# A four-layer graph network on one core: norm statistics aggregated on GpSimd, two additions turned into transfers, softmax masks and sums in operations of 1024 columns

## The chip, the core and the metric

The kernel runs on one core of a Trainium2 chip. The core has five engines that run side by side, each in the order of its own instructions, and wait for one another through semaphores. The profile calls them PE (TensorE, the matrix multiplier; PEld is its weight load), DVE (VectorE), ACT (ScalarE), POOL (GpSimd) and SP (which only issues transfers here). Transfers (DMA) are moved by 16 DMA engines; they are issued from SP or from POOL. The metric is the time on the device from the first to the last instruction of the core, in microseconds (us), as the median of the runs.

## The reference, cut to what matters

The input is 64 graphs of 256 nodes with 256 features each, and an adjacency matrix of 256 x 256 whole numbers for each graph. Four layers follow one another; around each there is a residual and a norm without gain or shift.

```python
x = _layernorm(x + transformer(x, adj))   # layer 0: 8 heads, masked softmax, feed-forward of 1024
x = _layernorm(x + gat1(x, adj))          # layer 1: graph attention
x = _layernorm(x + gat2(x, adj))          # layer 2: graph attention, then elu
x = _layernorm(x + relational(x, adj))    # layer 3: two graph convolutions

def transformer(x, adj, ...):
    qkv = x @ Wqkv.T + bqkv
    scores = jnp.where(allowed, (q * scale) @ k.T, -jnp.inf)
    attn = jax.nn.softmax(scores, axis=-1)
    x = _layernorm(x + (attn @ v) @ Wo.T + bo, ln1_g, ln1_b)
    ff = jax.nn.relu(x @ W1.T + b1) @ W2.T + b2
    return _layernorm(x + ff, ln2_g, ln2_b)

def _layernorm(x, axis=-1, eps=1e-5):
    m = jnp.mean(x, axis=axis, keepdims=True)
    v = jnp.var(x, axis=axis, keepdims=True)
    return (x - m) / jnp.sqrt(v + eps)
```

So there are six norms a graph: two in the transformer and one at the end of each layer. All is computed in 32-bit floating point.

## The kernel before

The program is built from small steps ("ops"). Each has an engine, an estimated cost, tiles that it reads and writes, and tiles come from rings of a fixed number of buffers. A list scheduler in the kernel file plays the ops of all 64 graphs through with these costs, and writes each engine's instructions in the order that comes out. About seven graphs are in flight at once: a graph's output leaves some 310 us after its input was transposed. `port="uses"` marks a VectorE op with two operands in SBUF; `port="waits"` marks a GpSimd op that the scheduler does not start while such an op runs. `lag` is the time from the end of an op to when its result is seen. `PERIOD` spaces the dates by which the graphs are due.

```python
RINGS = {..., "p": 12, "both": 4, "X": 8, "h": 3, "e": 3, "o": 4, ...}
class Plan:
    PERIOD = 46.0

def with_row(xt, row, op, reads=()):             # VectorE: xt op= row, 512 columns
    dve(0.60, lambda: nc.vector.tensor_tensor(xt(), xt(), row[:, None, :].to_broadcast([P, NB, D]), op=op), ...)

def add_later(xt, yt, reads):                    # a transfer that adds: issued by GpSimd
    op("POOL", 0.6, lambda: nc.gpsimd.dma_start(xt(), yt(), accum_op=ALU.add), [xt, *reads], [xt], lag=3.0)

def add(xt, yt):                                 # VectorE: xt += yt, 512 columns
    dve(0.60, lambda: nc.vector.tensor_tensor(xt(), xt(), yt(), op=ALU.add), [xt, yt], [xt], "uses")
```

The norm, used six times a graph. VectorE makes statistics of the two node tiles (`bn_stats`) and aggregates them to mean and variance (`bn_aggr`), GpSimd makes scale and shift of them in four small operations, and ScalarE applies these.

```python
def layer_norm(y):
    def stats():
        for i in range(NB):                      # NB = 2
            nc.vector.bn_stats(stat()[:, i, :], y()[:, i, :])
        for i in range(NB):
            nc.vector.bn_aggr(mv()[:, i, :], stat()[:, i, :])
    def root():
        nc.gpsimd.tensor_scalar(rstd()[:, 0, :], mv()[:, :, 1], 1.0, EPS, op0=ALU.mult, op1=ALU.add)
        nc.gpsimd.tensor_tensor(rstd()[:, 0, :], rstd()[:, 0, :], neghalf[:, 0:NB], op=ALU.pow)
        nc.gpsimd.tensor_tensor(rstd()[:, 1, :], mv()[:, :, 0], rstd()[:, 0, :], op=ALU.mult)
        nc.gpsimd.tensor_scalar(rstd()[:, 1, :], rstd()[:, 1, :], -1.0, 1.0, op0=ALU.mult, op1=ALU.mult)
    def apply():
        for i in range(NB):
            nc.scalar.activation(y()[:, i, :], y()[:, i, :], AF.Identity, bias=..., scale=...)
    dve(0.88, stats, [y], [mv, stat])
    op("POOL", 1.6, root, [mv], [rstd], port="waits", lag=0.4)
    act(1.0, apply, [y, rstd], [y])
```

The attention. For each half of the keys (`kt`) TensorE makes four banks of scores, one for each `r`, with two heads of 256 columns in a bank. ScalarE takes the exponential of a bank, VectorE multiplies it by the mask and later adds the two halves for the softmax sums.

```python
for kt in range(NB):
    ...                                          # scores of this half: 16 matmuls into 4 banks
    for r in range(4):
        act(0.58, lambda ...: nc.scalar.activation(pr(), sr(), AF.Exp, accum_out=...), [s[r]], [pr])
        dve(0.60, lambda ...: nc.vector.tensor_tensor(
            pr(), pr(), am()[:, kt, None, :].to_broadcast([P, KB, N]), op=ALU.mult), [pr, am], [pr], "uses")
for r in range(4):
    dve(0.60, lambda r=r: nc.vector.tensor_tensor(both[r](), p[0, r](), p[1, r](), op=ALU.add), ...)
for hg in range(KB):                             # sums (ones x both) and values (v x p): TensorE
    pe("col", 1.32, values, [v] + both + list(p.values()), [pc], [ctxT, inv])
    ...                                          # reciprocal of the sums and a product: VectorE
```

The feed-forward and the end of a graph:

```python
x1T = transposed(x1)                             # TensorE and ScalarE
with_row(x1, ln1g, ALU.mult)
with_row(x1, b2, ALU.add)                        # b2 here is ln1_b + b2
...                                              # x1T x W1, relu, x W2: 32 matmuls of 256 columns
y = product_plus(..., w2, NF, x1)                # VectorE adds x1 to the product
...
h = conv(conv(xt, 0, rel, rdeg), 1, rel, rdeg)
add(h, xt)                                       # the last residual
layer_norm(h)
op("SP", 0.4, lambda: nc.sync.dma_start(out_graph[g], h()), [h], [])
```

Of the kernel before, what the change touches and what calls it, by code (L numbers as in the profile page):

```python
# [12 lines left out]
AF = mybir.ActivationFunctionType  # L13
ALU = mybir.AluOpType
# [3 lines left out]
P = 128  # L18
EPS = 1e-5
# [5 lines left out]
SENT, BACK = 3.0, 4.5  # L25


RINGS = {"x": 3, "adj": 4, "bits": 2, "am": 2, "gm": 6, "T": 4, "qk": 2, "v": 2, "p": 12, "both": 4, "inv": 1, "ctxT": 2, "X": 8,
         "xr": 1, "hid": 1, "h": 3, "e": 3, "n": 1, "rel": 3, "hi": 2, "lo": 2, "o": 4, "blocks": 1, "turned": 1, "xT": 2}
DRAM = {"rows": 6}  # L30
SMALL = {"mv": 8, "st": 4, "rstd": 8, "r": 6, "rdeg": 4}
# [23 lines left out]
class Plan:  # L55
# [8 lines left out]
    TO = {"PE": 0.06, "POOL": 0.05}  # L64
    NEXT = {"DVE": 0.1}
    SWITCH = 0.1
    PERIOD = 46.0
    LAST, SPACE = 5, 0.1

    def __init__(self):  # L70
# [142 lines left out]
def tile_gnn_stack(ctx: ExitStack, tc: tile.TileContext, t: dict, out: bass.AP):  # L213
# [16 lines left out]
    nc = tc.nc  # L230
# [4 lines left out]
    KB = D // P  # L235
# [250 lines left out]
    def main_path(plan):  # L486
# [86 lines left out]
        def graph(g):  # L573
            def op(engine, cost, issue, reads, writes, takes=(), mode=None, port=None, lag=None):
                plan.op(engine, cost, issue, g, reads, writes, takes, mode, port, lag)

            def pe(mode, cost, issue, reads, writes, takes=()):
                op("PE", cost, issue, reads, writes, takes, mode)

            def dve(cost, issue, reads, writes, port=None):  # L580
                op("DVE", cost, issue, reads, writes, port=port)

            def act(cost, issue, reads, writes):
                op("ACT", cost, issue, reads, writes)

            def new(ring, shape, dtype=F32):
                return plan.tile(ring, shape, dtype)
# [9 lines left out]
            def with_row(xt, row, op, reads=()):  # L597
                dve(0.60, lambda: nc.vector.tensor_tensor(xt(), xt(), row[:, None, :].to_broadcast([P, NB, D]), op=op),
                    [xt, *reads], [xt], "uses")
# [8 lines left out]
            def add(xt, yt):  # L608
                dve(0.60, lambda: nc.vector.tensor_tensor(xt(), xt(), yt(), op=ALU.add), [xt, yt], [xt], "uses")
# [48 lines left out]

            def layer_norm(y):

                mv, stat = new("mv", [P, NB, 2]), new("st", [P, NB, 6])
                rstd = new("rstd", [P, 2, NB])

                def stats():
                    for i in range(NB):
                        nc.vector.bn_stats(stat()[:, i, :], y()[:, i, :])  # L666
                    for i in range(NB):
                        nc.vector.bn_aggr(mv()[:, i, :], stat()[:, i, :])  # L668

                def root():  # L670
                    nc.gpsimd.tensor_scalar(rstd()[:, 0, :], mv()[:, :, 1], 1.0, EPS, op0=ALU.mult, op1=ALU.add)  # L671
                    nc.gpsimd.tensor_tensor(rstd()[:, 0, :], rstd()[:, 0, :], neghalf[:, 0:NB], op=ALU.pow)  # L672
                    nc.gpsimd.tensor_tensor(rstd()[:, 1, :], mv()[:, :, 0], rstd()[:, 0, :], op=ALU.mult)
                    nc.gpsimd.tensor_scalar(rstd()[:, 1, :], rstd()[:, 1, :], -1.0, 1.0, op0=ALU.mult, op1=ALU.mult)  # L674

                def apply():
                    for i in range(NB):
                        nc.scalar.activation(y()[:, i, :], y()[:, i, :], AF.Identity, bias=rstd()[:, 1, i : i + 1],  # L678
                                             scale=rstd()[:, 0, i : i + 1])
# [29 lines left out]
            def projections(xT):  # L709
# [22 lines left out]
                act(0.47, lambda: nc.scalar.copy(v(), pv()), [pv], [v])  # L732
                return qk, v

            def attention(xT, am):

                qk, v = projections(xT)
                ctxT = new("ctxT", [P, KB, N])  # L740
                p = {}
                for kt in range(NB):
                    s = [new("bank", [P, KB, N]) for r in range(4)]
                    for r in range(4):
                        p[kt, r] = new("p", [P, KB, N])
# [8 lines left out]
                    pe("row", 0.97, scores, [qk], s, [p[kt, r] for r in range(4)])  # L754
                    for r in range(4):
                        pr, k = p[kt, r], 8 * g + 4 * kt + r
                        act(0.58, lambda pr=pr, k=k, sr=s[r]: nc.scalar.activation(  # L757
                            pr(), sr(), AF.Exp, accum_out=seen_sum[:, k : k + 1]), [s[r]], [pr])
                        dve(0.60, lambda pr=pr, kt=kt: nc.vector.tensor_tensor(  # L759
                            pr(), pr(), am()[:, kt, None, :].to_broadcast([P, KB, N]), op=ALU.mult), [pr, am], [pr], "uses")  # L760
                both = [new("both", [P, KB, N]) for r in range(4)]
                for r in range(4):
                    dve(0.60, lambda r=r: nc.vector.tensor_tensor(both[r](), p[0, r](), p[1, r](), op=ALU.add),  # L763
                        [p[0, r], p[1, r]], [both[r]], "uses")
                inv = new("inv", [P, KB, N])
                for hg in range(KB):
                    pc = new("bank", [P, 2, N])

                    def values(hg=hg, pc=pc):
                        for r in range(4):  # L770
                            nc.tensor.matmul(pc()[32 * r : 32 * r + 32, 1, :], lhsT=ones, rhs=both[r]()[:, hg, :],  # L771
                                             start=True, stop=True)
                        for kt in range(NB):
                            for r in range(4):
                                h = 4 * hg + r
                                nc.tensor.matmul(pc()[32 * r : 32 * r + 32, 0, :], lhsT=v()[:, kt, HD * h : HD * (h + 1)],  # L776
                                                 rhs=p[kt, r]()[:, hg, :], start=(kt == 0), stop=(kt == NB - 1))

                    pe("col", 1.32, values, [v] + both + list(p.values()), [pc], [ctxT, inv])
# [443 lines left out]
```

## Time and profile before

| what | value |
|---|---|
| median of 3 runs | 2897.77 us (2897.14 to 2898.14) |
| profiled execution | 2897.1 us |
| mean granted clock of TensorE | 0.991 of full speed |
| instructions with a place in the program | 50588 |
| transfers | 278.32 MB, 96 GB/s on average |

In the profile an engine's busy time is the time that is covered by its instructions, and its idle time before an instruction is put down to whatever ended last of what the instruction waited for. A row of a group of instructions gives line, engine, operation, the tile that is written and the tiles that are read, shapes (partitions x columns), the count, the sum of busy time, the mean of one in nanoseconds, and the idle time before them with what ended it. A row of the waits gives who waited for whom, the sum in us, how many times, and the longest. A row of a table of windows gives the stretch from the start of the span, its length, then the busy time of each engine in it with the count of instructions, the granted clock, the busy share of the DMA engines and GB/s. The chain of waits is followed back from the last instruction and is told in order of time: start, length, what. A matmul of 32-bit numbers is two matmul instructions in the profile. Instructions of one engine overlap somewhat in the records, so that the mean of one times the count can exceed the busy time.

### The profile page before, as it was taken

To read this page: it belongs to the slowest core of one execution; us is meant where nothing else is said; L and a number is where in the kernel's file an instruction comes from. 1 tells how busy PE (TensorE), PEld (TensorE's weight loads), DVE (VectorE), ACT (ScalarE), POOL (GpSimd) and SP (SyncE) were. 2 spreads that over 40 slices of the span, in tenths; PEclk is the share of its full clock that TensorE was granted. 3 is DMA by queue.
4 is the path that set the end of the run, shared out by engine and by line. 5 is a ranking of instruction groups with operands and counts; after the bars stand their busy time and mean duration, and the time that the engine had idled before them with its cause. 6 is when DMAs were issued, how large, how long until landed. Compare 5 with 4: busy or idle time off the path is not lost.

```text
span 2897.1 us, 50588 instructions
## 1 busy us (share of the span) xinstructions
PE 2805.3 (97%) x16182; PEld 2128.1 (73%) x16182; DVE 2523.0 (87%) x6557; ACT 1540.4 (53%) x3713; POOL 789.1 (27%) x1685
## 2 busy tenths in 40 slices
PE   8999999999999999999999999999999999999975
PEld 6776777777777767777777777777777777777853
DVE  6879899989989898999889898899888998999686
ACT  3555555546455555655555465555555655555343
POOL 2232223222223222222222322232231332222221
PEclk9999999999999999999999999999999999999998
DMA  7454455445444444454444544444444544443342
GB/s 183 81 108 88 99 101 102 89 101 102 95 92 100 87 94 94 98 101 93 104 97 93 98 99 99 100 91 102 86 93 96 109 88 93 105 90 72 67 83 70
DMA packets 844512, 278.32 MB, mean 96 GB/s; under 512 B 692656, under 2 KB 810672, under 8 KB 844240
## 3 DMA queue, kind: packets, MB, share of 16 engines
q1 hardware_dynamic: 808800, 240.27, 37.7%
q0 software_dynamic: 35440, 34.76, 8.5%
q8 instruction: 131, 2.15, 0.3%
q14 instruction: 141, 1.16, 0.1%
HBM read 157.43 MB, written 83.89 MB: 83 GB/s over the span
## 4 chain that ended last, share of the span: by engine, by line
PE 82%; DVE 10%; ACT 3%; DMA 2%; issue 2%; POOL 1%; SPq 1%; DVEq 0%; POOLq 0%; ACTq 0%
PE bank L657 67%; PE bank L919 4%; PE bank L776 3%; PE bank L751 3%; PE bank L771 2%; DMA rows<-turned 2%; DVE p L759 1%; PE bank L618 1%; DVE turned L629 1%; PE bank L839 1%; SPq L633 1%; DVE st L666 1%; DVE o L929 1%; DVE both L763 1%; DVE e L844 1%
## 5 line engine op out<-in xcount | busy, mean ns | idle before, releaser
L671 POOL TENSOR_SCALAR rstd<-mv 128x2 f32<-128x2 f32 x384 | 104.4, 272 | 1869.8 <-DVE mv L668 1496.7
L678 ACT ACTIVATE X<-X,rstd 128x256 f32<-128x256 f32 x640 | 349.8, 597 | 244.7 <-POOL rstd L674 230.1
L657 PE MATMUL bank<-cw,T 128*128 128x512 f32 x1024 | 467.9, 600 | 9.6 <-DMA T<-rows 9.1
L657 PE MATMUL bank<-T,w 128*128 128x256 f32 x2048 | 471.6, 380 | 5.2 <-ACT p L757 2.6
L657 PE MATMUL bank<-w,hid 128*128 128x256 f32 x2048 | 460.1, 380 | 0.0
L657 PEld LDWEIGHTS bank<-w,hid 128*128 128x128 f32 x2048 | 385.9, 190 | 62.7 <-issue 10.4
L657 PEld LDWEIGHTS bank<-T,w 128*128 128x128 f32 x2048 | 382.7, 190 | 64.5 <-issue 6.9
L757 ACT ACTIVATE p<-bank 128x512 f32<-128x512 f32 x512 | 299.9, 598 | 87.8 <-PE bank L751 87.6
L657 PEld LDWEIGHTS bank<-cw,T 128*128 128x128 f32 x1024 | 192.2, 192 | 209.3 <-issue 195.2
L759 DVE TENSOR_TENSOR p<-p,am 128x512 f32<-128x512 f32 x512 | 332.8, 680 | 10.8 <-ACT p L757 10.7
L672 POOL TENSOR_TENSOR rstd<-rstd,neghalf 128x2 f32<-128x2 f32 x384 | 305.7, 796 | 32.1
L809 ACT ACTIVATE hid<-bank,col_b 128x256 f32<-128x256 f32 x512 | 209.4, 474 | 113.8 <-PE bank L657 112.1
L657 PE MATMUL bank<-xT,wqkv 128*128 128x256 f32 x1024 | 251.6, 387 | 13.4 <-DVE xT L650 12.9
L657 PE MATMUL bank<-h,e 128*128 128x259 f32 x1024 | 253.8, 388 | 11.0 <-ACT e L849 9.3
L657 PE MATMUL bank<-gw,T 128*128 128x258 f32 x1024 | 249.1, 384 | 2.1 <-ACT inv L783 1.5
L657 PEld LDWEIGHTS bank<-h,e 128*128 128x128 f32 x1024 | 192.7, 192 | 66.6 <-issue 19.3
L666 DVE BATCH_NORM_STATS2 st<-X 128x6 f32<-128x256 f32 x640 | 237.5, 413 | 1.8
L906 ACT CAST hi<-bank 128x256 fp32r<-128x256 f32 x256 | 94.6, 370 | 263.4 <-PE bank L657 262.6
L657 PEld LDWEIGHTS bank<-xT,wqkv 128*128 128x128 f32 x1024 | 189.7, 192 | 54.0 <-issue 13.5
L780 DVE RECIPROCAL inv<-bank 128x256 f32<-128x256 f32 x128 | 220.0, 1734 | 8.8 <-PE bank L776 8.6
L657 PEld LDWEIGHTS bank<-gw,T 128*128 128x128 f32 x1024 | 191.1, 191 | 36.7 <-issue 5.2
L629 DVE STREAM_TRANSPOSE turned<-X 128x512 f32<-128x512 f32 x192 | 134.9, 703 | 45.0 <-DMA rows<-turned 23.0
(121 smaller groups left out, 4775.4 us busy)
## 6 DMA issues: line engine op xcount, KB each, us to landing
rows<-turned SPq DMA_DIRECT2D x1024, 64.0 KB, 2.2
T<-rows SPq DMA_DIRECT2D x256, 256.0 KB, 2.8
adj<-in_adj_dram SPq DMA_DIRECT2D x128, 256.0 KB, 3.0
blocks<-in_x_dram SPq DMA_DIRECT2D x512, 32.0 KB, 2.3
x<-in_x_dram SPq DMA_DIRECT2D x64, 256.0 KB, 3.0
xr<-in_x_dram SPq DMA_DIRECT2D x64, 256.0 KB, 2.8
xr<-row_ln_b POOLq DMA_DIRECT2D x64, 256.0 KB, 4.4
x<-row_bo POOLq DMA_DIRECT2D x64, 256.0 KB, 4.8
```

The source lines that it names most:

```text
L629: dve(0.63, lambda: nc.vector.transpose(turned().rearrange("p b q n -> p (b q n)"), xt().rearrange("p i (k b c) -> p b (i k) c", k=KB, b=4 ...
L657: nc.tensor.matmul(dst, lhsT=lhs(c), rhs=rhs(c), start=(c == 0), stop=(c == n - 1))
L666: nc.vector.bn_stats(stat()[:, i, :], y()[:, i, :])
L671: nc.gpsimd.tensor_scalar(rstd()[:, 0, :], mv()[:, :, 1], 1.0, EPS, op0=ALU.mult, op1=ALU.add)
L672: nc.gpsimd.tensor_tensor(rstd()[:, 0, :], rstd()[:, 0, :], neghalf[:, 0:NB], op=ALU.pow)
L678: nc.scalar.activation(y()[:, i, :], y()[:, i, :], AF.Identity, bias=rstd()[:, 1, i : i + 1], scale=rstd()[:, 0, i : i + 1])
L757: act(0.58, lambda pr=pr, k=k, sr=s[r]: nc.scalar.activation(pr(), sr(), AF.Exp, accum_out=seen_sum[:, k : k + 1]), [s[r]], [pr])
L759: dve(0.60, lambda pr=pr, kt=kt: nc.vector.tensor_tensor(pr(), pr(), am()[:, kt, None, :].to_broadcast([P, KB, N]), op=ALU.mult), [pr, am] ...
L780: dve(1.62, lambda hg=hg, pc=pc: nc.vector.reciprocal(inv()[:, hg, :], pc()[:, 1, :]), [pc], [(inv, hg)])
L809: act(0.36, lambda f=f, k=k, ph=ph: nc.scalar.activation(hid()[:, f + k, :], ph()[:, k, :], AF.Relu, bias=b1[:, f + k : f + k + 1]), [ph, ...
L906: act(0.27, lambda i=i, po=po: nc.scalar.copy(hi()[:, i, 0:D], po()[:, D:]), [po], [(hi, i)])
L919: nc.tensor.matmul(pa()[:, 0:n], lhsT=rel()[:, i, j * P : (j + 1) * P], rhs=part()[:, i, 0:n], start=(c == 0), stop=(c == len(terms) - 1))
```

## The change

The change takes work off VectorE in three ways.

The norm's two `bn_aggr` are left out. `bn_stats` leaves, for the even and the odd half of a row, a count, a mean and a sum of squared deviations; GpSimd now combines the halves itself, in nine small operations where there were four.

Two additions become transfers that add in place, issued by GpSimd: the row b2 onto x1 in the feed-forward, and the last residual, except in the last two graphs.

The masks and the sums of the softmax are made for two banks at a time: the tiles p and both hold twice as much, there are half as many of them, and each VectorE operation covers 1024 columns and not 512. The exponentials still come a bank at a time.

The scheduler's costs are set to the new shapes, and PERIOD goes from 46 to 47. No matmul is added or removed.

```diff
-RINGS = {... "p": 12, "both": 4, ...}
+RINGS = {... "p": 6, "both": 2, ...}
-    PERIOD = 46.0
+    PERIOD = 47.0
             def layer_norm(y):
-                mv, stat = new("mv", [P, NB, 2]), new("st", [P, NB, 6])
-                rstd = new("rstd", [P, 2, NB])
+                stat, t, rstd = new("st", [P, NB, 2, 3]), new("mv", [P, NB, 4]), new("rstd", [P, 2, NB])
                 def stats():
                     for i in range(NB):
-                        nc.vector.bn_stats(stat()[:, i, :], y()[:, i, :])
-                    for i in range(NB):
-                        nc.vector.bn_aggr(mv()[:, i, :], stat()[:, i, :])
+                        nc.vector.bn_stats(stat()[:, i].rearrange("p h k -> p (h k)"), y()[:, i, :])
                 def root():
...
+                    tensor_tensor(t()[:, :, 0:2], stat()[:, :, 0, 1:3], stat()[:, :, 1, 1:3], op=ALU.add)
+                    tensor_tensor(d, stat()[:, :, 0, 1], stat()[:, :, 1, 1], op=ALU.subtract)
+                    tensor_tensor(d, d, d, op=ALU.mult)
+                    tensor_scalar(s, s, 4 / D, 4 * EPS, op0=ALU.mult, op1=ALU.add)
+                    tensor_tensor(d, d, s, op=ALU.add)
+                    tensor_tensor(d, d, neghalf[:, 0:NB], op=ALU.pow)
+                    tensor_tensor(shift, m, d, op=ALU.mult)
+                    tensor_scalar(shift, shift, -1.0, 1.0, op0=ALU.mult, op1=ALU.mult)
+                    tensor_scalar(scale, d, 2.0, 1.0, op0=ALU.mult, op1=ALU.mult)
...
-                dve(0.88, stats, [y], [mv, stat])
-                op("POOL", 1.6, root, [mv], [rstd], port="waits", lag=0.4)
+                dve(0.56, stats, [y], [stat])
+                op("POOL", 2.5, root, [stat], [t, rstd], port="waits", lag=0.6)
...
-                        act(0.58, lambda pr=pr, k=k, sr=s[r]: nc.scalar.activation(
-                            pr(), sr(), AF.Exp, accum_out=seen_sum[:, k : k + 1]), [s[r]], [pr])
-                        dve(0.60, lambda pr=pr, kt=kt: nc.vector.tensor_tensor(
-                            pr(), pr(), am()[:, kt, None, :].to_broadcast([P, KB, N]), op=ALU.mult), [pr, am], [pr], "uses")
+                        act(0.58, lambda pr=pr, j=j, k=k, sr=s[r]: nc.scalar.activation(
+                            pr()[:, j], sr(), AF.Exp, accum_out=seen_sum[:, k : k + 1]), [s[r]], [(pr, j)])
+                        if j == 1:
+                            dve(1.14, lambda pr=pr, kt=kt: nc.vector.tensor_tensor(
+                                heads(pr), heads(pr), am()[:, kt, None, :].to_broadcast([P, 2 * KB, N]), op=ALU.mult),
+                                [pr, am], [pr], "uses")
-                both = [new("both", [P, KB, N]) for r in range(4)]
-                for r in range(4):
-                    dve(0.60, lambda r=r: nc.vector.tensor_tensor(both[r](), p[0, r](), p[1, r](), op=ALU.add),
+                for r in (0, 2):
+                    both[r] = new("both", [P, 2, KB, N])
+                    dve(1.14, lambda r=r: nc.vector.tensor_tensor(heads(both[r]), heads(p[0, r]), heads(p[1, r]), op=ALU.add),
...
-                with_row(x1, b2, ALU.add)
+                add_row_later(x1, b2)
...
-            add(h, xt)
+            if g < B - 2:
+                add_later(h, xt, [xt])
+            else:
+                add(h, xt)
             layer_norm(h)
```

More of the change, by code (lines that the diff above doesn't have):

```diff
@@ L25 @@
 SENT, BACK = 3.0, 4.5
-RINGS = {"x": 3, "adj": 4, "bits": 2, "am": 2, "gm": 6, "T": 4, "qk": 2, "v": 2, "p": 12, "both": 4, "inv": 1, "ctxT": 2, "X": 8,
+RINGS = {"x": 3, "adj": 4, "bits": 2, "am": 2, "gm": 6, "T": 4, "qk": 2, "v": 2, "p": 6, "both": 2, "inv": 1, "ctxT": 2, "X": 8,
          "xr": 1, "hid": 1, "h": 3, "e": 3, "n": 1, "rel": 3, "hi": 2, "lo": 2, "o": 4, "blocks": 1, "turned": 1, "xT": 2}
@@ L659, in layer_norm @@
             def layer_norm(y):
-                mv, stat = new("mv", [P, NB, 2]), new("st", [P, NB, 6])
-                rstd = new("rstd", [P, 2, NB])
+                stat, t, rstd = new("st", [P, NB, 2, 3]), new("mv", [P, NB, 4]), new("rstd", [P, 2, NB])
                 def stats():
                     for i in range(NB):
-                        nc.vector.bn_stats(stat()[:, i, :], y()[:, i, :])
-                    for i in range(NB):
-                        nc.vector.bn_aggr(mv()[:, i, :], stat()[:, i, :])
+                        nc.vector.bn_stats(stat()[:, i].rearrange("p h k -> p (h k)"), y()[:, i, :])
                 def root():
[L671 to L674, printed above, removed]
+                    tensor_tensor, tensor_scalar = nc.gpsimd.tensor_tensor, nc.gpsimd.tensor_scalar
+                    m, s, d = t()[:, :, 0], t()[:, :, 1], t()[:, :, 2]
+                    scale, shift = rstd()[:, 0, :], rstd()[:, 1, :]
+                    tensor_tensor(t()[:, :, 0:2], stat()[:, :, 0, 1:3], stat()[:, :, 1, 1:3], op=ALU.add)
[7 more added lines that the diff above has]
+                    tensor_scalar(scale, d, 2.0, 1.0, op0=ALU.mult, op1=ALU.mult)
                 def apply():
@@ L733, in projections, with heads @@
                 return qk, v
+            def heads(t):
+                return t().rearrange("p r k n -> p (r k) n")
             def attention(xT, am):
@@ L743, in attention @@
                     s = [new("bank", [P, KB, N]) for r in range(4)]
-                    for r in range(4):
-                        p[kt, r] = new("p", [P, KB, N])
+                    for r in (0, 2):
+                        p[kt, r] = new("p", [P, 2, KB, N])
                     def scores(kt=kt, s=s):
@@ L752, in scores @@
                                                  rhs=qk()[f, hg, :], start=True, stop=True)
-                    pe("row", 0.97, scores, [qk], s, [p[kt, r] for r in range(4)])
+                    pe("row", 0.97, scores, [qk], s, [p[kt, 0], p[kt, 2]])
                     for r in range(4):
-                        pr, k = p[kt, r], 8 * g + 4 * kt + r
-                        act(0.58, lambda pr=pr, k=k, sr=s[r]: nc.scalar.activation(
-                            pr(), sr(), AF.Exp, accum_out=seen_sum[:, k : k + 1]), [s[r]], [pr])
-                        dve(0.60, lambda pr=pr, kt=kt: nc.vector.tensor_tensor(
-                            pr(), pr(), am()[:, kt, None, :].to_broadcast([P, KB, N]), op=ALU.mult), [pr, am], [pr], "uses")
-                both = [new("both", [P, KB, N]) for r in range(4)]
-                for r in range(4):
-                    dve(0.60, lambda r=r: nc.vector.tensor_tensor(both[r](), p[0, r](), p[1, r](), op=ALU.add),
+                        pr, j, k = p[kt, r - r % 2], r % 2, 8 * g + 4 * kt + r
+                        act(0.58, lambda pr=pr, j=j, k=k, sr=s[r]: nc.scalar.activation(
[4 more added lines that the diff above has]
+                                [pr, am], [pr], "uses")
+                both = {}
+                for r in (0, 2):
+                    both[r] = new("both", [P, 2, KB, N])
+                    dve(1.14, lambda r=r: nc.vector.tensor_tensor(heads(both[r]), heads(p[0, r]), heads(p[1, r]), op=ALU.add),
                         [p[0, r], p[1, r]], [both[r]], "uses")
@@ L770, in values @@
                         for r in range(4):
-                            nc.tensor.matmul(pc()[32 * r : 32 * r + 32, 1, :], lhsT=ones, rhs=both[r]()[:, hg, :],
+                            nc.tensor.matmul(pc()[32 * r : 32 * r + 32, 1, :], lhsT=ones, rhs=both[r - r % 2]()[:, r % 2, hg, :],
                                              start=True, stop=True)
@@ L776, in values @@
                                 nc.tensor.matmul(pc()[32 * r : 32 * r + 32, 0, :], lhsT=v()[:, kt, HD * h : HD * (h + 1)],
-                                                 rhs=p[kt, r]()[:, hg, :], start=(kt == 0), stop=(kt == NB - 1))
-                    pe("col", 1.32, values, [v] + both + list(p.values()), [pc], [ctxT, inv])
+                                                 rhs=p[kt, r - r % 2]()[:, r % 2, hg, :], start=(kt == 0), stop=(kt == NB - 1))
+                    pe("col", 1.32, values, [v, *both.values(), *p.values()], [pc], [ctxT, inv])
                     dve(1.62, lambda hg=hg, pc=pc: nc.vector.reciprocal(inv()[:, hg, :], pc()[:, 1, :]), [pc], [(inv, hg)])
```

## The prediction

> **What bounds the kernel now.** I began with the page: busy shares, then the 40 slices.
>
> ```profile
> PE 2805.3 (97%) x16182; PEld 2128.1 (73%) x16182; DVE 2523.0 (87%) x6557; ACT 1540.4 (53%) x3713; POOL 789.1 (27%) x1685
> ...
> PE   8999999999999999999999999999999999999975
> ...
> DVE  6879899989989898999889898899888998999686
> ```
>
> TensorE is busy from the second slice to the 38th. VectorE, from which the change takes work, has eights and nines, but is not the fuller of the two. A busy TensorE need not be an efficient one, so I took the starts of its matmuls between 100 and 2700 us from the trace: a 128x256 matmul follows its predecessor by a median of 216 ns in all the large groups, and by 215 to 226 ns on average. What lies above the median in these groups sums to about 60 us, a few ns at each change of group. Matmuls stream; hardly any waits are hidden in the busy share. Next, the middle and the end as two windows (start and end, length, busy us of PE, PEld, DVE, ACT, POOL, clock, DMA share, GB/s):
>
> ```profile
> 100.00:2700.00 2600.00, 2570.24 (x15041) 1955.43 (x15035) 2325.29 (x6016) 1426.73 (x3459) 723.61 (x1536) 1.00 0.47 95
> 2700.00:2898.00 198.00, 149.11 (x574) 103.21 (x572) 133.65 (x410) 75.15 (x155) 39.11 (x102) 0.91 0.36 74
> ```
>
> This is the reading on which most rests. In the middle TensorE idles for 2600 - 2570 = 30 us, 1.1%. In the last 198 us it idles for 49, and in the first 100 for 14 (one wait of 12.9 us for the first transposed input, which the change leaves as it is). These 93 us are all the idle time there is. Who ends it in the middle is told by the waits of TensorE there (sum, count, longest):
>
> ```profile
> PE bank L657 <- ACT p L757: 7.2, 8, 1.6
> PE bank L839 <- DVE h L830: 3.4, 1, 3.4
> PE bank L771 <- DVE both L763: 3.1, 5, 1.2
> ```
>
> Small, rare, of many kinds; VectorE ends some directly and stands behind others. The end is different: there the chain runs through VectorE, ScalarE, transfers and short matmuls in turn. Its last norm shows the part that the change rebuilds:
>
> ```profile
> 2888.13 0.49 DVE st L666 x2
> 2888.62 0.18 issue
> 2888.80 0.31 DVE mv L668 x2
> 2889.15 0.10 issue
> 2889.26 0.20 POOL rstd L671
> 2889.46 0.07 issue
> 2889.53 0.71 POOL rstd L672
> ```
>
> L668 is the aggregation that goes; each small GpSimd operation takes 0.20 us and 0.07 of issue, the power 0.71.
>
> **What the Trainium skill says.** (1) "Trainium Kernel Development and Optimization", section Performance Expectations: matmul busy time is a bad measure of the distance to the roofline, because matmuls are pipelined. The trace agrees in part: one matmul is recorded at 380 ns where 216 pass to the next. So I used the pace for the middle. (2) "VectorE: DVE Perf Modes", section Why `tensor_tensor` can't do 2×_2P or 4×: both read ports are taken, so 32-bit operations on two tensors gain no speed from length, only one fixed cost. The rows below agree: 413 ns at 256 columns, 680 at 512. (3) "GPSIMD Engine Reference", section 8, Key points: GpSimd shares its SBUF interfaces with VectorE and contends with VectorE instructions that have two SBUF inputs. The trace agrees: single durations of L673 have a median of 197 ns but a 90th percentile of 602, and in the timeline such an operation ends where a VectorE operation on two SBUF tensors ends. (4) "DMA: Bandwidth & Descriptors", section Rules for kernel authors: a transfer that accumulates is to be issued from GpSimd. Here all adding transfers stand in GpSimd's queue; each takes it 1.3 us and lands after 4.4 to 4.8.
>
> **The change, part by part.** The groups:
>
> ```profile
> L759 DVE TENSOR_TENSOR p<-p,am 128x512 f32<-128x512 f32 x512 | 332.8, 680 | 10.8 <-ACT p L757 10.7
> L763 DVE TENSOR_TENSOR both<-p 128x512 f32<-128x512 f32 x256 | 167.5, 681 | 0.0
> L668 DVE BATCH_NORM_AGGREGATE mv<-st 128x2 f32<-128x6 f32 x768 | 115.5, 174 | 1.0
> L875 DVE SCALAR_TENSOR_TENSOR n<-n,X 128x256 f32<-128x256 f32 x128 | 53.0, 414 | 0.0
> L598 DVE TENSOR_TENSOR X<-X,row_b 128x512 f32<-128x512 f32 x64 | 43.7, 682 | 0.1
> L609 DVE TENSOR_TENSOR o<-o,X 128x512 f32<-128x512 f32 x64 | 43.6, 682 | 0.2
> L671 POOL TENSOR_SCALAR rstd<-mv 128x2 f32<-128x2 f32 x384 | 104.4, 272 | 1869.8 <-DVE mv L668 1496.7 <-DVE r L854 127.0 <-ACT p L757 61.7
> L672 POOL TENSOR_TENSOR rstd<-rstd,neghalf 128x2 f32<-128x2 f32 x384 | 305.7, 796 | 32.1
> ```
>
> VectorE loses: the aggregations, 115.5 us. The b2 row, 43.7. The last residual in 62 of 64 graphs, 43.6 x 62/64 = 42.2. Masks and sums: 256 more columns cost 680 - 414 = 266 ns, so 1024 columns take 680 + 2 x 266 = 1212 ns. The 768 old operations keep it busy 500.3 us, 651 ns each with their overlap; 384 new ones at 651 + 532 = 1183 ns make 454. That is 46 less. Sum: 115.5 + 43.7 + 42.2 + 46 = 247 us. VectorE goes to 2523 - 247 = 2276 us, 79% of a span near 2880.
>
> GpSimd gains: five small operations in each of 384 norms, at the mean of 272 ns: 5 x 384 x 0.272 = 522 us. 64 + 62 = 126 more transfers at 1.29 us: 163. It goes to 789 + 685 = 1474 us, 51%. The four operations of a norm, from first start to last end, take 1.53 us undisturbed and 1.86 on average in the trace; nine take 1.86 + 5 x (0.272 + 0.084 of gap) = 3.64, and with masks that block it for 1.2 and not 0.6 us perhaps 4.
>
> A norm's way from statistics to scale grows by 5 x 0.356 = 1.78 us and loses the aggregation, about 0.34: 1.4 us net, 8.6 a graph. A graph spends about 310 us in flight among seven, so in the middle this is 3% more to be covered by other graphs, not time on the path. The b2 transfer (issue 1.3, landing some 4.6 us later) lies beside the 32 matmul instructions with W1 and the 32 with W2 (2048 of each in the page for 64 graphs) that stand before the addition of x1, 64 x 0.216 = 13.8 us: hidden. The last residual has only the output behind it: hidden in the middle, and kept off the last two graphs. Transfers: the present adding ones take 8.5% of the 16 engines; as many again makes the DMA share some 55%, no bound.
>
> On the path that sets the end: TensorE's instructions are the same, 2805 us. In the middle I expect a less loaded VectorE to take away some half of the 30 us of idle time, -15, and a little of the 60 us at changes of group, -5. In the last 157 us VectorE is busy for some 117: 38 aggregations of 0.15 and up to 4 residuals of 0.65 come off, 8 us, of which perhaps half counts where it is the one waited for, -4. Against it two or three norms of the last graph are in the chain, +1.4 each, +4. Start: 0. Sum: -20, to 2897 - 20 = 2877; I take 2879, for the coarser operations.
>
> **The rivals.** First, GpSimd becomes the bound that VectorE was. It is in order: a transfer waiting for x1 or h holds up the norms of other graphs behind it, and with 1.2 us masks a chain of nine can stretch to 6 us and more. For it: ScalarE already waits 294 us for the scale (next lines), and 63 us of GpSimd's idle time is a transfer's issue waiting for its input.
>
> ```profile
> ACT X L678 <- POOL rstd L674: 230.1, 125, 9.6
> ...
> ACT o L678 <- POOL rstd L674: 64.3, 30, 5.7
> ```
>
> Against it: GpSimd would stand at 51%, and ScalarE at 53% can afford waits. It would make the time 2910 to 2960. Second, the relief is simply hidden: TensorE sets the pace, VectorE's idle time grows by what it lost, and the time stays at 2890 to 2900. The 98.9% in the middle speaks for it. Third, VectorE was the real pacemaker, in the drain above all, and nearly all of the middle's idle time and 10 to 15 us of the end go: 2850 to 2860. VectorE at 89% in the middle speaks for it; that it waits 99 us for one TensorE product (L792 for L657) speaks against.
>
> **Range and chances.** To gain 2% the time must fall under 2840, so 58 of the 93 idle us must go, 14 of which are the start's: 5%. To lose 2% it must pass 2956, so TensorE's idle time in the middle must triple; only the first rival does that: 4%. Within 2%: 91%. The range runs from the third rival's good end to a mild form of the first: 2852 to 2910.
>
> **What would show it.** Right: VectorE's busy time near 2276 and 1024-column operations near 1212 ns; no L668 group; GpSimd near 1474 and its chain 3.6 to 4 us; PE busy within 10 us of 2805; PE idle between 100 and 2700 us about 15 us; the end's idle time within 5 us of 49. Wrong: PE waits in the middle for ScalarE's X or T behind GpSimd's rstd (first rival), idle time in the middle unchanged (second), or an end shorter by 10 us (third).

## The result, and the profile after

The changed kernel takes 3018.84 us (median of 4 runs, 3016.74 to 3021.59). The ratio to the kernel before is 1.0419, with a 95% interval of 1.0401 to 1.0437. The change costs 121 us, where the prediction said 2879 and ended its range at 2910.

The page of the kernel after, the lines of busy shares and slices that were shown of before:

```profile
PE 2855.1 (95%) x16182; PEld 2141.4 (71%) x16182; DVE 2365.2 (78%) x5279; ACT 1535.7 (51%) x3713; POOL 1441.5 (48%) x3731
...
PE   7999999899999999999999999999999999999976
...
DVE  5778777778778879788788787878878877698586
```

VectorE has lost 158 us of work and its slices have fallen from eights and nines to sevens and eights. GpSimd has gone from 27% to 48%. TensorE has the same 16182 instructions, but is recorded as busy for 50 us more. The span grew by 122.7 us: those 50, and 73 of more idle time. The two windows tell where:

```profile
100.00:2700.00 2600.00, 2500.58 (x14348) 1880.03 (x14347) 2081.21 (x4634) 1356.06 (x3288) 1276.64 (x3271) 0.99 0.53 103
2700.00:3020.00 320.00, 273.22 (x1339) 196.55 (x1337) 231.93 (x557) 142.67 (x327) 133.37 (x395) 0.94 0.43 85
```

In the middle TensorE idles for 99 us in 2600 instead of 30, and gets through 14348 matmuls where it did 15041. The loss is spread over the whole middle. In the last 200 us of the span it idles for 46 us, as before (48), and in the first 100 for 19 (14).

The 50 us of longer busy time are not a slower pace throughout. A large part is the granted clock. The trace has 20 stretches, 104 us in all, in which TensorE was granted half its clock; before it had 10, of 53 us. In them one 128x256 matmul follows another after a median of 427 ns, outside them after 216 in both kernels. TensorE is recorded as busy for 80 and 35 us of these stretches; half of the difference, about 22 us, is an estimate of what the clock adds. In the middle the stretches went from two (7 us) to nine (44 us), and seven of the nine begin during a stall of TensorE of 2.3 us or more, or within 1 us of its end. A window that holds one of 3.4 us and one of 10.2 us, so that its mean clock is 0.93:

```profile
500.00:600.00 100.00, 90.85 (x509) 66.64 (x508) 77.64 (x170) 50.53 (x124) 47.67 (x130) 0.93 0.47 95
```

Some 14 us more are the last matmuls before a wait: such a one is recorded with its whole 380 ns and not with the 216 to the next, and TensorE's waits went from 79 to 164 (an estimate: 85 x 0.164 us). The rest is not taken apart.

The longest waits of TensorE in the middle (100 to 2800 us) of the kernel after:

```profile
PE bank L761 <- ACT qk L732: 11.3, 6, 6.2
PE bank L657 <- ACT p L767: 10.6, 8, 4.1
PE bank L657 <- DMA T<-rows: 10.2, 11, 2.8
```

The first was not in the list of before at all. The copies of the queries and keys out of PSUM (two instructions on L732) are 0.81 us of work on ScalarE, an engine at 51%. They are late because ScalarE, which goes strictly by its order, stands before them. What ScalarE waits for, first of the kernel after (230.1 and 64.3 us before):

```profile
ACT X L685 <- POOL rstd L681: 384.7, 214, 9.2
ACT o L685 <- POOL rstd L681: 84.7, 46, 5.5
```

The longest single stall of TensorE in the middle, 6.18 us, shows the mechanism. These are lines of the timeline of the kernel after, engine by engine: start, length, what, and idle time before it with what ended that.

```profile
564.33 1.96 PE L657 MATMUL bank<-wqkv,xT 128*128 128x256 f32 x8
572.48 2.09 PE L761 MATMUL bank<-qk 32*128 32x256 f32 x16 [6.18 <-ACT qk L732]
```

```profile
565.68 1.09 ACT L685 ACTIVATE o<-o,rstd 128x256 f32<-128x256 f32 x2 [1.44 <-POOL rstd L681]
...
568.30 0.20 ACT L767 ACTIVATION_READ_ACCUMULATOR p<-bank 128x1 f32 x1
570.97 1.09 ACT L685 ACTIVATE X<-X,rstd 128x256 f32<-128x256 f32 x2 [2.48 <-POOL rstd L681]
571.97 0.81 ACT L732 ACTIVATE qk<-bank,col_bqkv 128x256 f32<-128x256 f32 x2
```

```profile
566.85 0.70 POOL L678 TENSOR_TENSOR mv<-mv,neghalf 128x2 f32<-128x2 f32 x1
567.62 1.03 POOL L679 TENSOR_TENSOR rstd<-mv 128x2 f32<-128x2 f32 x1
568.74 1.06 POOL L680 TENSOR_SCALAR rstd<-rstd 128x2 f32<-128x2 f32 x1
569.77 1.17 POOL L681 TENSOR_SCALAR rstd<-mv 128x2 f32<-128x2 f32 x1
```

```profile
567.38 2.38 DVE L770 TENSOR_TENSOR p<-p,am 128x1024 f32<-128x1024 f32 x2 [0.62 <-ACT p L767]
569.67 1.22 DVE L776 TENSOR_TENSOR both<-p 128x1024 f32<-128x1024 f32 x1
```

Read from the bottom. VectorE runs three operations of 1024 columns in a row. The last three of GpSimd's nine, 0.19 us each when undisturbed, get in only at the borders of these and take over 1 us each. So the scale is 2.5 us late for ScalarE, which has the copy of qk behind it in its order; and TensorE, whose next matmuls want qk, waits. These 2.5 us are not all of the 6.18: just before, ScalarE had stood 1.44 us for the scale of another norm, and between the two waits it does other work that stands ahead of the copy in its order. ScalarE, GpSimd and VectorE are far from full over the span (51%, 48% and 78%).

### The profile page after: what moved, and what is told of

Read it like the earlier page. It is cut to its first block, busy times and chain, and to the rows that moved or that the text cites. A ratio compares the mean times of both kernels' runs of the same rounds, so it can differ in the third digit from the quotient of the medians.

```text
span 3019.8 us, 51049 instructions
## 1 busy us (share of the span) xinstructions
PE 2855.1 (95%) x16182; PEld 2141.4 (71%) x16182; DVE 2365.2 (78%) x5279; ACT 1535.7 (51%) x3713; POOL 1441.5 (48%) x3731
## 5 line engine op out<-in xcount | busy, mean ns | idle before, releaser
L673 POOL TENSOR_TENSOR mv<-st 128x4 f32<-128x4 f32 x384 | 148.6, 387 | 979.2 <-DVE st L665 864.5
L657 PE MATMUL bank<-T,w 128*128 128x256 f32 x2048 | 479.0, 385 | 8.9 <-ACT T L621 4.4
L657 PEld LDWEIGHTS bank<-T,w 128*128 128x128 f32 x2048 | 389.1, 193 | 75.2 <-issue 11.1
L770 DVE TENSOR_TENSOR p<-p,am 128x1024 f32<-128x1024 f32 x256 | 307.1, 1214 | 46.7 <-ACT p L767 46.5
L678 POOL TENSOR_TENSOR mv<-mv,neghalf 128x2 f32<-128x2 f32 x384 | 307.4, 800 | 30.1
```

The costliest lines, as they stand in the source:

```text
L657: nc.tensor.matmul(dst, lhsT=lhs(c), rhs=rhs(c), start=(c == 0), stop=(c == n - 1))
L673: tensor_tensor(t()[:, :, 0:2], stat()[:, :, 0, 1:3], stat()[:, :, 1, 1:3], op=ALU.add)
L678: tensor_tensor(d, d, neghalf[:, 0:NB], op=ALU.pow)
L770: dve(1.14, lambda pr=pr, kt=kt: nc.vector.tensor_tensor(heads(pr), heads(pr), am()[:, kt, None, :].to_broadcast([P, 2 * KB, N]), op=ALU.m ...
```

## The experiments

Four theories stood at the start. N: the norm's longer way over GpSimd costs the time. T: the adding transfers do. M: the operations of 1024 columns do. O: only the new order does, which the scheduler makes anew whenever a cost changes. N was then split in two. S: norms come later than the scheduler reckons, and the engines, whose order it has fixed by that reckoning, stand waiting. L: the length of the chain and GpSimd's queue cost it in any order. All ratios are to the kernel before, run beside the experiment on the same chip.

### One part at a time

**The norm alone** (statistics without aggregation, nine operations on GpSimd, costs of the change; PERIOD 46):

```diff
-                dve(0.88, stats, [y], [mv, stat])
-                op("POOL", 1.6, root, [mv], [rstd], port="waits", lag=0.4)      # four operations
+                dve(0.56, stats, [y], [stat])
+                op("POOL", 2.5, root, [stat], [t, rstd], port="waits", lag=0.6) # nine operations
```

> The kernel before with the norm part alone (no aggregation on VectorE, nine small GpSimd operations a norm). Theory N (the longer GpSimd chain, behind which other norms' chains queue, is what costs the 121 us): slower by 60 to 110 us, PE idle in 100 to 2700 us at 60 us or more, and the time from the end of the statistics to the chain's first operation near 1 us as after. Theory T (the transfers that add, above all the last residual, whose landing takes longer than the scheduler reckons): within 15 us of before. Theory M (operations of 1024 columns block GpSimd and delay the matmuls): within 15 us. Theory O (only the new order and PERIOD): any sign, under 30 us.

Measured: 2972.08 us, ratio 1.0263 (1.0246 to 1.0280): 75 us of the 121. TensorE idles 62 us in the middle. ScalarE waits 443 us for the scale, where it was 294. The larger row of the two, 230.1 before:

```profile
ACT X L685 <- POOL rstd L681: 358.9, 209, 9.4
```

**The last residual alone**:

```diff
-            add(h, xt)
+            if g < B - 2:
+                add_later(h, xt, [xt])
+            else:
+                add(h, xt)
```

> The kernel before with the last residual added by a transfer in 62 graphs, nothing else. Theory T: slower by 30 to 90 us, VectorE waiting for the transfer before the statistics of o by 30 us or more in total. Theory N: within 15 us of before. Theory M: within 15 us. Theory O: any sign, under 30 us.

Measured: 2907.86 us, ratio 1.0037 (1.0024 to 1.0049): 11 us. VectorE does wait for the landing before the statistics of o, 35 times and 35.1 us, but little of it reaches the end. T falls as the main cause.

**b2 alone**:

```diff
-                with_row(x1, b2, ALU.add)
+                add_row_later(x1, b2)
```

> The kernel before with b2 added to x1 by a transfer, nothing else. Theory T: slower by up to 30 us, less than the last residual, as some 14 us of matmuls lie between. Theories N and M: within 15 us of before, rather faster, as VectorE loses 44 us. Theory O: any sign, under 30 us.

Measured: 2897.34 us, ratio 1.0000 (0.9991 to 1.0009). The transfer is hidden, and so is what it takes off VectorE.

**Masks and sums of 1024 columns alone**:

```diff
-                            pr(), pr(), am()[:, kt, None, :].to_broadcast([P, KB, N]), op=ALU.mult), ...      # for each r
+                                heads(pr), heads(pr), am()[:, kt, None, :].to_broadcast([P, 2 * KB, N]), ...  # for r = 1 and 3
```

> The kernel before with masks and softmax sums in operations of 1024 columns, nothing else. Theory M: slower by 40 us or more, GpSimd's four small operations stretched from 1.86 us to over 2.3 on average, matmuls waiting for sums or for banks. Theories N and T: within 15 us of before. Theory O: any sign, under 30 us.

Measured: 2902.52 us, ratio 1.0020 (1.0010 to 1.0030): 6 us slower, and the four operations take 1.92 us on average, not over 2.3. M falls as the main cause. The four sum to 93 us of 121.

### The same norm in three orders

**The scheduler told 3.4 us** for the nine operations. They take 3.5 from first start to last end on average (3.47 in the run of the norm alone).

```diff
-                op("POOL", 2.5, root, [stat], [t, rstd], port="waits", lag=0.6)
+                op("POOL", 3.4, root, [stat], [t, rstd], port="waits", lag=0.6)
```

> The norm part alone (2972 us, where before is 2897), with the scheduler told 3.4 us for the nine operations and not 2.5. Theory S (the scheduler reckons the chain too short, so that engines in their fixed order stand waiting for norms that are late): most of the loss comes back, 2885 to 2915 us, and ScalarE waits less for the scale. Theory L (nine operations a norm on one in-order engine cost that much whatever the order, because chains of different graphs queue behind one another): 2950 us or more.

Measured: 2912.39 us, ratio 1.0043 (1.0030 to 1.0056). One number in the cost table, and 60 of the 75 us are back. The instructions are the same as in the norm alone; only their order differs. The waits of ScalarE in this run:

```profile
ACT X L685 <- POOL rstd L681: 193.0, 112, 8.4
ACT o L685 <- POOL rstd L681: 51.4, 20, 8.1
```

The way from the first statistics to the first application of the scale, taken from the starts in the trace, is 3.61 us on average in the kernel before, 5.23 with the norm alone, and 6.10 here. The longest way belongs to nearly the fastest of the three. So it isn't the length of the way that costs, but engines standing before its end: ScalarE stands before the scale in 155 of the 384 norms before, in 248 with the norm alone, and in 132 here. L falls.

**The costs of before** (0.88 and 1.6), so that all engines keep the order of before:

```diff
-                dve(0.56, stats, [y], [stat])
-                op("POOL", 2.5, root, [stat], [t, rstd], port="waits", lag=0.6)
+                dve(0.88, stats, [y], [stat])
+                op("POOL", 1.6, root, [stat], [t, rstd], port="waits", lag=0.4)
```

> The norm part alone with the costs that the scheduler had before (0.88 and 1.6 us), so that every engine keeps the order of the kernel before. Were it the new order alone that costs (theory O): near 2897 us. Theory S: slower than the norm part with 2.5, as the gap between reckoned and real grows from 1.0 to 1.9 us: 2985 to 3030. Theory L: near 2970.

Measured: 3075.35 us, ratio 1.0610 (1.0593 to 1.0628). The direction is that of S, but the time lies 45 us beyond its range. O is out: the old order is the worst of the three for this norm.

```profile
ACT X L685 <- POOL rstd L681: 526.2, 269, 10.5
```

**The dose without the relief**: the kernel before, with VectorE's aggregation and with its order, and five idle multiplications after GpSimd's four operations:

```diff
                     nc.gpsimd.tensor_scalar(rstd()[:, 1, :], rstd()[:, 1, :], -1.0, 1.0, op0=ALU.mult, op1=ALU.mult)
+                    for _ in range(5):
+                        nc.gpsimd.tensor_scalar(rstd()[:, 1, :], rstd()[:, 1, :], 1.0, 1.0, op0=ALU.mult, op1=ALU.mult)
```

> The kernel before in its own order, with VectorE's aggregation kept and five more small operations (times 1.0) at the end of GpSimd's four: the chain gets as long as after, without relief for VectorE. Theories S and L: 70 to 130 us slower, GpSimd busy near 1310 us. If GpSimd's length is not the cause (then it is the missing aggregation that changed the order, or the statistics' reading): within 20 us of before.

Measured: 3208.41 us, ratio 1.1067 (1.1048 to 1.1085): 310 us, far beyond the 130 that S and L both allowed. GpSimd is at 39%, TensorE idles for 196 us of the middle, and ScalarE's wait is 813 us in all:

```profile
ACT X L680 <- POOL rstd L676: 648.7, 282, 11.7
```

### The other way

**Two GpSimd operations and not four**: adding EPS and turning the mean's sign go into one VectorE operation (which also moves the mean by EPS); the scheduler is told so.

```diff
+                    nc.vector.scalar_tensor_tensor(mv(), mv(), EPS, sgn, op0=ALU.add, op1=ALU.mult)
-                    (the first and the last tensor_scalar of root)
-                dve(0.88, ...); op("POOL", 1.6, ...)
+                dve(1.0, ...);  op("POOL", 1.0, ...)
```

> The other way: two GpSimd operations a norm and not four; adding EPS and turning the mean's sign go into one small VectorE operation (it also moves the mean by EPS, 1e-5), and the scheduler is told 1.0 us each. VectorE gets some 55 us more to do. If the length of GpSimd's chain is what counts (S or L, some 75 us for 1.6 us more): 0.7 us less gives 10 to 30 us, 2867 to 2887. If VectorE is what bounds beside TensorE: slower, 2905 or more.

Measured: 2916.93 us, ratio 1.0073 (1.0056 to 1.0090). A miss for the theory in its plain form: where the reckoning is about right (1.4 us for 1.18 measured), a shorter chain brings nothing. VectorE has 60 us more to do (2583), and the time is 19 us longer. That VectorE bounds beside TensorE, as the change assumed, is not shown by this: the order is new too, and the next run shows that a new order alone can cost more.

**A reserve in the reckoning**: the kernel before, with 2.5 us reckoned for its four operations, which take 1.86.

```diff
-                op("POOL", 1.6, root, [mv], [rstd], port="waits", lag=0.4)
+                op("POOL", 2.5, root, [mv], [rstd], port="waits", lag=0.4)
```

> The kernel before with one number changed: the scheduler is told 2.5 us for the four operations, where they take 1.86 and it was told 1.6. Theory S in its plain form (time is lost only where a norm comes later than reckoned): ScalarE's wait for the scale falls below 200 us and the time lies between 2875 and 2900 us. If a reckoned reserve costs as much as a shortfall: 2910 or more.

Measured: 2928.37 us, ratio 1.0103 (1.0087 to 1.0120), with ScalarE's wait for the scale down to 177 us. S in its plain form, too late costs and too early is free, does not hold: a reserve of 1 us costs 29 us. TensorE's idle time goes from 30 to 48 us, in small waits for many engines.

### Taking parts out of the change, and telling it the true costs

**The change without its norm part** (the norm and costs of before; all else of after):

```diff
-                dve(0.56, stats, [y], [stat])                                   # and nine operations
-                op("POOL", 2.5, root, [stat], [t, rstd], port="waits", lag=0.6)
+                dve(0.88, stats, [y], [mv, stat])                               # with aggregation, and four operations
+                op("POOL", 1.6, root, [mv], [rstd], port="waits", lag=0.4)
```

> The kernel after with the norm of before (aggregation on VectorE, four GpSimd operations, their old costs); transfers, wide operations and PERIOD 47 stay. If the parts add up (residual +11, b2 +1, masks +6): near 2915 us, so that the norm is 104 of the 121 us. If transfers or masks cost more beside one another: 2930 or more.

Measured: 2929.84 us, ratio 1.0112 (1.0091 to 1.0133). The norm is 89 us of the 121. The rest costs 31 us together, where residual, b2 and masks alone sum to 18.

**The change with the true cost of the nine operations** (one number):

```diff
-                op("POOL", 2.5, root, [stat], [t, rstd], port="waits", lag=0.6)
+                op("POOL", 3.4, root, [stat], [t, rstd], port="waits", lag=0.6)
```

> The kernel after with one number changed: the scheduler is told 3.4 us for the nine operations and not 2.5. Theory S (what costs is that norms come later than the fixed order of the engines reckons with): at least 60 us back, 2900 to 2955 us, and ScalarE's wait for the scale falls from 469 us to under 300. Theory L (length of the chain, or GpSimd's queue): 3000 us or more.

Measured: 2941.86 us, ratio 1.0157 (1.0140 to 1.0174): 77 us back, ScalarE's wait for the scale 276 us and not 469.

**And the costs of the adding transfers**, as measured for those of a row in the kernel after, which take GpSimd 1.3 to 1.4 us and land 4.3 to 5.0 us after the start of the issue (medians of the three groups):

```diff
-                op("POOL", 0.6, lambda: nc.gpsimd.dma_start(xt(), yt(), accum_op=ALU.add), [xt, *reads], [xt], lag=3.0)
+                op("POOL", 1.3, lambda: nc.gpsimd.dma_start(xt(), yt(), accum_op=ALU.add), [xt, *reads], [xt], lag=3.4)
```

> As the last, and the scheduler is also told what transfers that add take: 1.3 us to issue and 3.4 to land, for 0.6 and 3.0. Theory S: another 10 to 40 us, 2870 to 2925 us, near or below the kernel before, and VectorE waits less for the residual's landing. Theory L: no better than the last.

Measured: 2912.08 us, ratio 1.0045 (1.0028 to 1.0062). Three numbers in the cost table bring back 107 of the 121 us, with no operation of the change taken out. VectorE's wait for the landing of the residual falls from 44.4 us in the run before this one (39.6 in the kernel after) to 18.7. For the residual's own transfer these 4.7 us are a reserve: in the kernel after it takes GpSimd 0.97 us, and lands after 3.8 us at the median (3.3 to 6.8), where 3.6 were reckoned.

### What the last 13 us are

"True costs" stands for the version just shown, 3.4 for the norm and 1.3 and 3.4 for the transfers.

**True costs, the residual on VectorE again:**

```diff
-            if g < B - 2:
-                add_later(h, xt, [xt])
-            else:
-                add(h, xt)
+            add(h, xt)
```

> The change with true costs (2912 us), the last residual added on VectorE in all graphs. If the residual's landing before the statistics is what remains: 2890 to 2902 us. If not: 2905 to 2920.

Measured: 2918.06 us, ratio 1.0068 (1.0051 to 1.0085). Not the residual.

**True costs, masks and sums of 512 columns:**

```diff
-RINGS = {... "p": 6, "both": 2, ...}          # and dve(1.14, ...) for two banks
+RINGS = {... "p": 12, "both": 4, ...}         # and dve(0.60, ...) for each bank, as before
```

> The change with true costs (2912 us), masks and sums in operations of 512 columns again. If wide operations block GpSimd's small ones and make its chain vary: chain shorter than 3.4 us on average, 2890 to 2905 us. If not: 2905 to 2920.

Measured: 2903.86 us, ratio 1.0019 (1.0010 to 1.0028): 8 us better, close to the 6 of the masks alone. But the chain did not get shorter (3.50 us on average in both runs), so that the reason expected is not the right one.

**True costs, only the norm and b2 of the change, PERIOD 46:**

```diff
-    PERIOD = 47.0
+    PERIOD = 46.0
...                                             # masks and sums of 512 columns, as in the last
-            if g < B - 2:
-                add_later(h, xt, [xt])
-            else:
-                add(h, xt)
+            add(h, xt)
```

> The change with true costs, without the last residual's transfer and the wide masks, PERIOD 46: what stays is the norm on GpSimd and b2 by a transfer. If the long chain on GpSimd is what remains: 2905 to 2920 us. If residual and masks are: 2885 to 2900, at or below the kernel before.

Measured: 2888.98 us, ratio 0.9967 (0.9954 to 0.9979). This version beats both kernels, by 10 us against before. How much of this is the relief of VectorE, and how much a better order, is not shown.

```profile
PE 2801.7 (97%) x16182; PEld 2127.7 (74%) x16182; DVE 2414.5 (84%) x5725; ACT 1537.3 (53%) x3713; POOL 1367.1 (47%) x3669
```

GpSimd is as loaded as after (47%), its chain as long (3.49 us on average), and TensorE idles 27 us in the middle.

**The change without its norm part, with these costs for the transfers:**

```diff
-                op("POOL", 0.6, ..., [xt, *reads], [xt], lag=3.0)      # the norm of before, all else of after
+                op("POOL", 1.3, ..., [xt, *reads], [xt], lag=3.4)
```

> The change without its norm part (2930 us), with true costs for the transfers. Theory S (late landings against a fixed order): 2890 to 2912 us, and VectorE waits less than 53 us for the landing before the statistics. If the transfers themselves cost it: 2920 or more.

Measured: 2949.58 us, ratio 1.0178 (1.0160 to 1.0197): 20 us slower than with the old ones, and outside the range of S. The wait for the landing did go, from 52.7 us to 1.4, as S expected, but the new order has another fault, which one line of TensorE's waits in the middle holds (2.6 us before):

```profile
PE bank L657 <- ACT T L621: 43.0, 24, 2.0
```

**PERIOD**: the change with true costs at 46, and the kernel before at 47.

```diff
-    PERIOD = 47.0          # the change with true costs
+    PERIOD = 46.0
```

```diff
-    PERIOD = 46.0          # the kernel before
+    PERIOD = 47.0
```

> The change with true costs (2912 us), PERIOD 46 and not 47. If PERIOD 47 is what costs the rest: 2890 to 2902 us. If PERIOD matters little: 2905 to 2920; any other value means that the order alone moves the time by more than the parts do.

> The kernel before with PERIOD 47. If PERIOD costs time by itself: 2907 to 2920 us. If not: within 8 us of before.

Measured: 2921.29 us, ratio 1.0072 (1.0055 to 1.0088), 9 us over the same at 47; and 2898.53 us, ratio 0.9994 (0.9985 to 1.0002). PERIOD is no cause of the loss. The move of the order that it makes was worth 9 us in one program and nothing in the other. Together with the 29 us of the reserve and the 20 us of the longer transfer costs, both by a new order of the same instructions, this means that a difference of 10 us, and even of 30, between two orders cannot be put down to a part on one pair of runs.

## Why the prediction was wrong, point by point

| reckoned: cost + lag, us | chain measured, us | ScalarE's wait for the scale, us | PE idle, 100 to 2700 us | time, us | which |
|---|---|---|---|---|---|
| 2.0 | 1.86 | 294 | 30 | 2897 | before |
| 3.1 | 3.47 | 443 | 62 | 2972 | norm alone |
| 3.1 | 3.52 | 469 | 99 | 3019 | after |
| 2.0 (and 0.88 for statistics) | 3.32 | 652 | 131 | 3075 | norm alone, old costs |
| 2.0 | 3.50 | 813 | 196 | 3208 | before, five more |
| 2.9 | 1.87 | 177 | 48 | 2928 | before, reserve |
| 4.0 | 3.52 | 244 | 37 | 2912 | norm alone, 3.4 |
| 4.0 | 3.50 | 225 | 41 | 2912 | after, true costs |
| 4.0 | 3.49 | 183 | 27 | 2889 | norm, b2, true costs |

**The bound.** Right in the figures: TensorE's 30 us of idle time in the middle is all that there was to gain, and the relief of VectorE is worth little; with true costs, the norm part and b2 only 10 us are won. Wrong in what it meant for a loss. A TensorE at 98.9% was read as one that sets its own pace, so that the others have slack. But the others have only the slack that the order leaves them, and that order was made for the durations of this very program. The dose experiment shows it: in an unchanged order, 1.6 us more a norm on an engine with 70% of its time free cost 310 us.

**The step that failed** is this one: "in the middle this is 3% more to be covered by other graphs, not time on the path", and with it, under the first rival, "ScalarE at 53% can afford waits". Where each engine's order is written down beforehand, another graph covers a delay only as far as that order happens to allow: of the dose's 384 x 1.64 = 630 us about half reached the end. ScalarE's next instruction may be a copy for quite another graph, but it stands behind the application of a scale. What covers a longer norm is an order that reckons with it. In the order with 3.4 us the way of a norm is longer than in the losing one, 6.10 us against 5.23, and 60 of the 75 us are back. I read the new cost of 2.5 us in the diff, worked out 3.64 for the same thing, and did not hold the two against each other. Against 2.5 + 0.6 stood 3.64 to 4.

**The first rival** had the right engine and nearly the right place: its mark, waits behind rstd, is what the trace shows. Its grounds were only half right. It spoke of GpSimd becoming the bound. At 47% in the fastest version and 48% in the slow one, GpSimd is not the bound. Its queue is there: from the end of the statistics to the chain's first operation pass 1.02 us on average in the kernel after, mostly behind the chains of other graphs; but 1.12 in the fastest version. 4% was far too little for it: no number of mine spoke against it but busy shares. Its sum was right: TensorE's idle time in the middle did have to triple, and it went from 30 to 99 us.

**Sizes that held.** The 1024-column operation: 1212 predicted, 1212 to 1214 measured:

```profile
L770 DVE TENSOR_TENSOR p<-p,am 128x1024 f32<-128x1024 f32 x256 | 307.1, 1214 | 46.7 <-ACT p L767 46.5
```

GpSimd: 1474 us predicted, 1441 measured. The chain: 3.64 to 4, measured 3.52. The start and the end: no change to speak of, as said. b2: hidden, as said.

**Sizes that did not.** VectorE went to 2365 us, not 2276. The terms were busy times of single groups, and neighbouring instructions overlap in the records by some 80 ns (after an operation of 680 ns the next one starts at 0.60 us), so a removed instruction frees its spacing, not its duration. An aggregation is 174 ns long, but the next instruction starts after 110 on average. The runs of one part each show VectorE's busy time fall by 67 us with the norm (115.5 predicted), 32 with b2 (43.7), 30 with the residual (42.2) and 17 with masks and sums (46): 145 in all and not 247. The last residual was "hidden in the middle"; alone it costs 11 us. VectorE, also in a fixed order, waits 35 us for landings that take 3.8 us at the median but up to 7.5, where the scheduler reckons 3.6 from the start of the issue. PE's busy time was to stay within 10 us of 2805 and rose by 50; the half clock and the matmuls before stalls, worked out above, make some 36 of these.

**What stays open.** Why a reserve of 1 us costs 29 us in the kernel before, and why the longer transfer costs, a reserve for the residual too, made an order with 43 us of waits for T. Both are properties of orders that the scheduler finds, and no run here takes them apart. S gave the right direction in the four runs that made a norm's estimate too short or mended it, but its range held in only three of the eight runs for which it named one. The dose with a mended estimate, and estimates between 2.5 and 3.4 us, were not run, so that 3.4 is a value that works and not one shown to be the best. Of the 13 us that the full change with true costs loses to before, 8 went with the masks and sums of 1024 columns, which cost 6 alone; but differences of this size between two orders prove little, and the rest stays open. Why the granted clock is halved beside long stalls is not shown either: the trace shows only that they go together.

## What to carry to other kernels

Where engines run in an order that was fixed beforehand by estimated durations, the busy share of an engine says little of the slack that a longer operation on it has: compare the estimate in the schedule with the duration that the trace allows you to expect, operation by operation, and mend the estimate before judging the change. Here a step that occurs 384 times was reckoned at 3.1 us and took 3.5; reckoning 4.0 brought 60 us back. But too large an estimate costs as well: one of 2.9 for 1.9 us cost 29. And a removed instruction gives back its start-to-start spacing, not its duration.

## What the runs showed of the hardware that was not expected

A GpSimd operation on two numbers a partition takes 0.19 us alone (the power 0.70), but up to 1.2 us beside a single VectorE operation of 1024 columns with two operands in SBUF, and each small operation of a chain can meet the next such one: three in a row took 3.3 us in the timeline above. The border between two such operations is no sure way in: of the 3072 small operations other than the power, 43 take over 1.25 us, and one is recorded at 4.7 us beside four of 1024 columns in a row. The Trainium skill states the contention ("GPSIMD Engine Reference", section 8, Key points), and the prediction had it, as a mean. The mean of a small operation moved from 272 to 303 ns only. It is the tail that a fixed order meets: 9 in 10 chains of the kernel after end within 5.1 us, one takes 9.2, and the median is 3.1. The fastest version has much the same tail (4.8 us for 9 in 10, 7.2 at most) in an order that reckons 4.0, so the tail alone is not what costs.
